# The last 22 expert blocks in another order, transposes of y behind the next first product, and a combine without gates

## The chip, the cores and the metric

The kernel runs on one core of a Trainium2 chip as one launch. The metric is the device time of the launch in microseconds; of the kernel before there are three runs: 2601.29, 2603.02 and 2605.94 us, so the median is 2603.02. A further run was recorded by the hardware profiler and gives all views of the profile below.

## The reference

Four sequences (B = 4) of T = 512 tokens of width C = 512 go through two layers, each with two residual steps:

```python
x = x + mamba2(gate(x))        # layer 0, state space block
x = x + experts(gate(x))       # layer 0, 8 experts, top 2
x = x + attention(gate(x))     # layer 1, 16 heads in 4 groups
x = x + swiglu(gate(x))        # layer 1, 1408 wide, ternary weights
```

`gate` is a bidirectional recurrence over the tokens: two scans forward and two backward (a numerator and a denominator, a*decay + input), whose quotient, scaled, multiplies sigmoid(x). Its inputs besides x are the same for every step, so the quotient (called a gate below) of a layer's step and a batch can be computed before x is there.

The experts: every token gets 8 logits, keeps the two largest, and weights the two experts' outputs by a softmax over the two.

```python
for e in range(E):
    h = x @ w1[e].T + b1[e]
    y = h[:, 0::2] * sigmoid(1.702 * h[:, 0::2]) * (h[:, 1::2] + 1.0)
    out += (y @ w2[e].T + b2[e]) * we[:, None]      # we: 0 where e isn't chosen
```

So a token needs two experts only, and 4 * 512 * 2 = 4096 rows of work are there in all. By these inputs the experts 0 to 7 get 445, 1766, 393, 17, 483, 772, 163 and 57 rows.

## The kernel before

**Blocks.** Rows with one expert are gathered in blocks of 128. There are NBLK = 39 blocks. The first NEARLY = 17 (early blocks) are full blocks of the first three batches to come out of the state space layer, and run beside that layer's last batch. The 22 late blocks hold what is left; FIRST = 15 of them may hold rows of batch 0 and stand ahead of the others, so that batch 0 is complete before the last blocks. `order_blocks` (L604 to L659) makes the lists: from the counts of rows it gives each block in use a rank (the number of used blocks ahead of it, by a product with a triangular matrix), compares that rank with the numbers 0, 1, 2, ... along the free axis (`lane`, L640) and multiplies the one-hot result with token lists and experts. The rank thus is the position in the order of work, and experts stand in the order of their numbers.

**A round.** `Experts.round` (L816 to L839) handles block i: it fetches the rows of block i+3 by an indirect DMA on POOL (`fetch`, L722), asks for weights (`weights`, L745 on, `load_w1` L696 and L701, `load_w2` L707 and L708, all on SP's queue), transposes the rows (`flip`: TensorE `pfl` L734, ACT copies `hT` L736), runs the first product (`pg` L763), the down product of block i−2 (`po` L796, then DVE L801 and a scatter of rows on POOL, L802), transposes the next block's rows, and runs the second product (`pn` L774). Between them ACT and DVE make y (tanh L121, DVE L768, L778, L780, L781). `finish` transposes y (`pyt` L787) and ACT copies it to `yT` (L789), which the down product reads. All products are fp32 with 512 columns; each of four matmuls appears in the trace as two records.

**Weights.** An expert's load is two halves of w1 (1 MB each), b1 (0.5 MB), w2 (1 MB) and b2 (0.25 MB). Early blocks use one buffer set (slot 0). Late blocks alternate two slots by the block's number (`slot`), block 17 on slot 1, block 18 on slot 0. A load is conditional: it moves nothing where the slot holds the expert already.

```python
kw = {"cond": e != self.held[s]} if s in self.held else {}
```

**Gates.** `make_gates` and `gate_pair` (L218 to L364) compute the gates of layer 1 for two halves of the features at a time, a pair, as a generator. `pump` runs one step of it; `more` (L1464) calls it after each round, and attention calls `nudge` in every head. A batch's gate must be whole when `gated` needs it; whatever is missing is made then.

**Order.** The program's text gives most of the order on each engine; a recording layer merges what stands under `after(...)` into the streams named there, where it fits. Behind block 31 `load_group(0)` puts attention's first weights on SP's queue (L1418, L1424). The results of batch 0 are read back by POOL (`rr`, L1435), scaled and added on ACT (L1442) and DVE (L1443), transposed (`pcb`, L1448) and added to x (L1452), one quarter of 128 tokens in each of four of the last five rounds (L1480 to L1488). Batches 1 to 3 are combined the same way in the first heads of attention (L1643 to L1645), where SP issues the reads. Attention starts with keys `pk` (L1530).

Of the kernel before, what the change touches and what calls it, by code (L numbers as in the profile page):

```python
# [10 lines left out]
F32 = mybir.dt.float32  # L11
I32 = mybir.dt.int32
AF = mybir.ActivationFunctionType
ALU = mybir.AluOpType
# [3 lines left out]
P = 128  # L18
B, T, C = 4, 512, 512
NC = C // P  # L20
NT = T // P
# [14 lines left out]
NBLK = (B * T * TOPK + E * (P - 1)) // P  # L36
NROW = B * T * TOPK + 1

NEARLY = -(-((B - 1) * T * TOPK - E * (P - 1)) // P)

FIRST = (T * TOPK + E * (P - 1)) // P
# [39 lines left out]
def block_kernel(ctx: ExitStack, tc: tile.TileContext, a: dict, out: bass.AP):  # L81
    nc = tc.nc

    @contextmanager
    def after(*engines):

        with ExitStack() as es:
            for e in engines:
                last = next(
                    (i for i in reversed(nc.cur_bb.bb.instructions) if i.engine == e.engine), None  # L90
                )
                if last is not None:
                    es.enter_context(tc.issue_after(last))
            yield
# [39 lines left out]
    rt = ctx.enter_context(tc.tile_pool(name="moe_r", bufs=1))  # L134
    tmp = ctx.enter_context(tc.tile_pool(name="tmp", bufs=2))
# [23 lines left out]
    def row(name):  # L159
# [10 lines left out]
                            pattern=[[1, P]], channel_multiplier=-1)  # L170
    tri_gt = const.tile([P, P], F32, name="tri_gt")
    nc.gpsimd.affine_select(out=tri_gt, in_=ones, compare_op=ALU.is_gt, fill=0.0, base=0,
                            pattern=[[-1, P]], channel_multiplier=1)
# [5 lines left out]
    th = const.tile([P, B], F32, name="th")  # L179
# [189 lines left out]
    def pump(n=1, until=None):  # L369
        for _ in range(n):  # L370
            while until not in made and not next(making, True):
                pass
# [18 lines left out]
    def gated(l, b, xb, pool, part=slice(0, T), **kw):  # L391
# [23 lines left out]
                            pattern=[[1, E], [-1, E]], channel_multiplier=0)  # L415
# [3 lines left out]
                            pattern=[[1, P]], channel_multiplier=-1)  # L419
# [3 lines left out]
                            pattern=[[-NQ, E]], channel_multiplier=1)  # L423
    nc.gpsimd.affine_select(out=sel, in_=sel, compare_op=ALU.is_ge, fill=0.0, base=NQ - 1,
                            pattern=[[NQ, E]], channel_multiplier=-1)

    def count(name, pattern, mult=0, base=0):
        n = 1
        for _, k in pattern:
            n *= k  # L430
        ti = tmp.tile([P, n], I32, tag="th", name=f"{name}_i")
        nc.gpsimd.iota(ti, pattern=pattern, base=base, channel_multiplier=mult)
        tf_ = rt.tile([P, n], F32, name=name)
        nc.vector.tensor_copy(tf_, ti)
        return tf_

    lane = count("lane", [[1, P]])

    res_id = [count(f"res{c}", [[TOPK * T, B], [P, NT]], 1, 1 + c * T) for c in range(2)]
    for r in res_id:  # L440
        for b in (0, B - 1):
            rb = r[:, b * NT : (b + 1) * NT]
            nc.vector.tensor_scalar(rb, rb, float(AT[b] - b * TOPK * T), None, ALU.add)
    e_nq = count("e_nq", [[NQ, E]])
    v_id = count("v_id", [[1, 1]], 1)

# [157 lines left out]
    def order_blocks(lo, hi):  # L604

        n = hi - lo
        cv = rt.tile([P, 1], F32, tag="cv", name="cv")
        nc.vector.tensor_tensor(jk, sel, cnt[:, (N2 if lo else N2 - NT), :], ALU.mult)
        nc.vector.tensor_reduce(cv, jk, AX.X, ALU.add)
        use = rt.tile([P, 1], F32, tag="use", name="use")  # L610
        if lo == 0:
            nc.vector.scalar_tensor_tensor(use, v_lo, float(P), cv, ALU.add, ALU.is_le)
        else:
            nc.vector.tensor_tensor(use, v_lo, cv, ALU.is_lt)
            nc.vector.tensor_tensor(use, use, taken, ALU.subtract)
        pi = ps_tp("pidx")
        rank = rt.tile([P, 1], F32, tag="vrank", name="vrank")
        if lo == 0:
            nc.tensor.matmul(pi[:, P : P + 1], lhsT=tri_lt, rhs=use, start=True, stop=True)
            nc.vector.tensor_copy(rank, pi[:, P : P + 1])  # L620
        else:

            two = rt.tile([P, 2], F32, tag="two", name="two")
            nc.vector.tensor_tensor(jk, sel, cnt[:, NT, :], ALU.mult)
            nc.vector.tensor_reduce(rank, jk, AX.X, ALU.add)
            nc.vector.tensor_scalar(two[:, 0:1], v_lo, rank, use, ALU.is_lt, ALU.mult)
            nc.vector.tensor_tensor(two[:, 1:2], use, two[:, 0:1], ALU.subtract)
            nc.tensor.matmul(pi[:, P : P + 2], lhsT=tri_lt, rhs=two, start=True, stop=True)
            nc.tensor.matmul(pi[:, P + 2 : P + 3], lhsT=ones, rhs=two[:, 0:1], start=True, stop=True)

            nc.vector.tensor_scalar(
                rank, pi[:, P + 1 : P + 2], pi[:, P + 2 : P + 3], two[:, 1:2], ALU.add, ALU.mult
            )
            nc.vector.scalar_tensor_tensor(
                rank, pi[:, P : P + 1], two[:, 0:1], rank, ALU.mult, ALU.add
            )
        if lo == 0:
            nc.vector.scalar_tensor_tensor(taken, rank, float(n), use, ALU.is_lt, ALU.mult)
        of = tmp.tile([P, NBLK], F32, tag="th", name="of")
        nc.vector.tensor_scalar(of[:, :n], lane[:, :n], rank, use, ALU.is_equal, ALU.mult)  # L640
        nc.tensor.matmul(pi[:, :n], lhsT=toks, rhs=of[:, :n], start=True, stop=True)
        nc.tensor.matmul(pi[0:1, 2 * P : 2 * P + n], lhsT=v_e, rhs=of[:, :n], start=True, stop=True)

        gf = tmp.tile([P, NBLK], F32, tag="th", name="gf")
        nc.vector.tensor_scalar(gf[:, :n], pi[:, :n], NROW - 2.0, None, ALU.add)
        nc.vector.tensor_copy(idx_h[:, lo:hi], gf[:, :n])
        low = tmp.tile([P, NBLK], I32, tag="th", name="low")
        nc.vector.tensor_scalar(
            low[:, :n], idx_h[:, lo:hi], T - 1, (B - 1) * T, ALU.bitwise_and, ALU.bitwise_xor
        )  # L650
        nc.vector.tensor_scalar(
            idx_h[:, lo:hi], idx_h[:, lo:hi], 1, (B - 1) * T,
            ALU.logical_shift_right, ALU.bitwise_and,
        )
        nc.vector.tensor_tensor(idx_h[:, lo:hi], idx_h[:, lo:hi], low[:, :n], ALU.bitwise_xor)
        ef = tmp.tile([1, NBLK], F32, tag="th", name="ef")
        nc.vector.tensor_scalar(ef[:, :n], pi[0:1, 2 * P : 2 * P + n], E - 1.0, None, ALU.add)
        nc.vector.tensor_copy(eb[:, lo:hi], ef[:, :n])
        nc.vector.tensor_copy(idx_o[:, lo:hi], pi[:, :n])  # L659

    class Experts:
# [154 lines left out]
        def round(self):  # L816
            i = self.i
            self.fetch(i + self.LOOK)
            if i < NBLK:
                self.weights(i)  # L820
                if i >= NEARLY:
                    self.weights(i + 1)
                self.flip(i)
                half = self.first_half(i)
                next(half)
                if i + 1 < NEARLY:
                    self.weights(i + 1, True)
            if i >= 2:
                self.down(i - 2)
            self.second_weights(i - 2)  # L830
            if i < NBLK:
                self.flip(i + 1)
                self.y[i] = next(half)
                if i + 1 < NEARLY:
                    self.more_weights(i + 1)
            if i - 1 in self.y:
                with after(nc.tensor):
                    self.yT[i - 1] = self.finish(self.y.pop(i - 1))
            self.i += 1  # L839

    moe = Experts()
# [617 lines left out]
    with tc.tile_pool(name="moe_w2", bufs=1, reuse_waits="tile") as wm:  # L1459
        moe.add_slot(wm)  # L1460
        for b in range(B):
            nc.sync.dma_start(out=x[b], in_=xs_d[b])

        def more(limit):  # L1464
            while moe.i < min(limit, moe.known):
                moe.round()
                with after(nc.vector):
                    pump()

        more(moe.i + 1)  # L1470
        next(routing)
        more(moe.i + 1)
        next(routing)
        more(moe.i + 1)
        order_blocks(NEARLY, NBLK)
        moe.know(NBLK)
        more(NBLK - 8)
        first_group = load_group(0)

        more(min(NEARLY + FIRST + 2, NBLK - NT - 1))  # L1480
        results = {t: load_results(0, t, nc.gpsimd) for t in range(2)}
        more(moe.i + 1)
        for t in range(NT):
            more(moe.i + 1)
            with after(nc.tensor, nc.vector, nc.scalar):
                add_results(0, t, results.pop(t))
            if t + 2 < NT:
                results[t + 2] = load_results(0, t + 2, nc.gpsimd)  # L1488
        assert moe.i == NBLK
        early_h = gated(2, 0, x[0], wa, tag="wq", name="h2_0")  # L1490
        moe.round()
        moe.round()
# [281 lines left out]
```

## Time and profile before

| | |
|---|---|
| median of three runs | 2603.02 us |
| profiled execution | 2605.88 us, its span 2604.2 us |
| granted TensorE clock, mean | 0.979 |
| TensorE busy | 2450.3 us, 94% |
| VectorE (DVE) / ScalarE (ACT) / GpSimd (POOL) busy | 1412.3 / 1033.2 / 259.9 us |
| moved by DMA | 259.82 MB, 231.51 MB of it on the queue that SP uses |
| first late block, first product | 897.08 us |
| first matmul of attention | 1185.96 us |

The span is the time from the first to the last record; the launch's own time is some 1.7 us more. Views of the trace give lines of start, length, engine, source line, operation, output and inputs, and in brackets the idle time before it with what ended it. A wait belongs to the instruction that waited; instructions of one engine run in order, so what stands behind a waiting instruction waits too.

### The profile page before, as it was taken

How to read it: one execution, taken by the hardware profiler on the slowest of the kernel's cores; microseconds unless marked ns; L12 is line 12 of the kernel's file. 1: busy time of each engine (PE TensorE's matmuls, PEld its weight loads, DVE VectorE, ACT ScalarE, POOL GpSimd, SP SyncE). 2: the span in 40 equal slices, each digit the busy share in tenths (PEclk: the TensorE clock that was granted, in tenths of full speed). 3: DMA queues.
4: the chain of work that ended last, by engine and by line, in shares of the span. 5: the costliest groups of instructions: out<-in, count | busy, mean ns of one | idle time of the engine just before them, and what ended most of it. 6: DMA issues, size and time to landing. Idle time of an engine off the chain costs nothing.

```text
span 2604.2 us, 24554 instructions
## 1 busy us (share of the span) xinstructions
PE 2450.3 (94%) x8204; PEld 1300.7 (50%) x8204; DVE 1412.3 (54%) x2788; ACT 1033.2 (40%) x2126; POOL 259.9 (10%) x299
## 2 busy tenths in 40 slices
PE   3889998999989999989999999999999999999999
PEld 1555555556544444435555555555555554444444
DVE  8798898996345565556666654556553441011010
ACT  4576757666123233224454444345443431000000
POOL 1031223322211121210000000000000000000000
PEclk9989999999899999999999999999999999999999
DMA  6222423324244697876221101111000012000000
GB/s 216 82 93 94 166 74 126 130 69 146 82 177 170 217 371 296 334 242 219 61 65 45 45 29 29 45 41 33 21 25 16 17 53 97 17 0 16 8 8 16
DMA packets 91391, 259.82 MB, mean 100 GB/s; under 512 B 9857, under 2 KB 19457, under 8 KB 80641
## 3 DMA queue, kind: packets, MB, share of 16 engines
q1 hardware_dynamic: 82080, 231.51, 25.5%
q0 software_dynamic: 6880, 22.55, 2.4%
q10 hardware_dynamic: 2304, 4.20, 0.4%
q8 instruction: 65, 1.06, 0.2%
q14 instruction: 62, 0.50, 0.1%
HBM read 284.82 MB, written 47.05 MB: 127 GB/s over the span
## 4 chain that ended last, share of the span: by engine, by line
PE 77%; DVE 14%; ACT 4%; DMA 3%; issue 2%; POOL 0%; SPq 0%; ACTq 0%; DVEq 0%; POOLq 0%
PE pd L1616 8%; PE pq L1552 7%; PE pfu L1683 6%; PE pfo L1693 6%; PE pfg L1678 6%; PE pctx L1601 5%; PE pn L774 5%; PE pg L763 5%; PE po L796 4%; PE pc L995 4%; PE psc L1569 3%; PE po L1223 3%; PE pv L1538 2%; PE ptp L1592 2%; PE pk L1530 2%; PE pz L1066 2%
## 5 line engine op out<-in xcount | busy, mean ns | idle before, releaser
L1552 PE MATMUL pq<-h,wq 128*128 128x512 f32 x512 | 249.4, 603 | 9.5 <-ACT pr L1579 9.4
L1616 PE MATMUL pd<-cx,wd 128*128 128x512 f32 x512 | 222.4, 592 | 0.0
L995 PE MATMUL pc<-h,wxb 128*128 128x512 f32 x320 | 150.0, 624 | 45.8 <-DVE h L1263 38.7
L1687 ACT ACTIVATE hd<-pfg,cols 128x512 f32<-128x512 f32 x44 | 30.3, 688 | 381.0 <-PE pfg L1678 381.0
L1688 DVE SCALAR_TENSOR_TENSOR hd<-pfu,cols,hd 128x512 f32<-128x512 f32 x44 | 33.0, 751 | 269.2 <-PE pfu L1683 269.1
L1572 DVE TENSOR_TENSOR psc<-psc,mask 128x128 f32<-128x128 f32 x256 | 71.7, 287 | 196.1 <-PE psc L1569 196.0
L1579 ACT ACTIVATE pr<-psc,nmax 128x128 f32<-128x128 f32 (+3 forms) x256 | 135.3, 529 | 98.1 <-DVE nmax L1574 97.3
L1601 PE MATMUL pctx<-pT,v 128*128 128x512 f32 (+3 forms) x512 | 155.9, 448 | 7.5 <-ACT pT L1595 4.0
L1683 PE MATMUL pfu<-h,ffu 128*128 128x512 f32 x352 | 158.7, 592 | 0.9 <-DMA ffu<-in_upT 0.9
L1678 PE MATMUL pfg<-h,ffg 128*128 128x512 f32 x352 | 158.6, 592 | 0.0
L796 PE MATMUL po<-w,yT 128*128 128x512 f32 x312 | 145.3, 607 | 12.7 <-ACT yT L789 12.7
L1569 PE MATMUL psc<-kT,qT 128*128 128x128 f32 (+3 forms) x512 | 151.8, 436 | 2.2 <-ACT qT L1560 1.2
L1616 PEld LDWEIGHTS pd<-cx,wd 128*128 128x128 f32 x512 | 96.1, 190 | 114.8 <-issue 110.5
L1693 PE MATMUL pfo<-hd,ffd 128*128 128x512 f32 x352 | 151.7, 592 | 0.0
L763 PE MATMUL pg<-w,hT 128*128 128x512 f32 x312 | 145.1, 605 | 6.7 <-DMA w<-in_w1x 6.7
L1601 PEld LDWEIGHTS pctx<-pT,v 128*128 128x128 f32 x512 | 94.6, 193 | 99.2 <-issue 37.4
L774 PE MATMUL pn<-w,hT 128*128 128x512 f32 x312 | 141.0, 593 | 1.7 <-DMA w<-in_w1x 1.7
L1624 DVE TENSOR_TENSOR xr<-xr,pd 128x512 f32<-128x512 f32 x64 | 44.0, 688 | 175.5 <-PE pd L1616 175.5
L1574 DVE TENSOR_REDUCE nmax<-psc 128x1 f32<-128x128 f32 (+3 forms) x256 | 123.4, 484 | 2.7
L1552 PEld LDWEIGHTS pq<-h,wq 128*128 128x128 f32 x512 | 87.8, 193 | 68.4 <-issue 57.4
L1592 PEld LDWEIGHTS ptp<-ident,pr 128*128 128x128 f32 x640 | 78.3, 143 | 86.9 <-issue 40.4
L995 PEld LDWEIGHTS pc<-h,wxb 128*128 128x128 f32 x320 | 61.8, 199 | 118.2 <-issue 73.0
(305 smaller groups left out, 4217.4 us busy)
## 6 DMA issues: line engine op xcount, KB each, us to landing
w<-in_w1x SPq DMA_DIRECT2D x80, 1024.0 KB
w<-in_w2x SPq DMA_DIRECT2D x40, 1024.0 KB
wb<-in_b1x SPq DMA_DIRECT2D x40, 512.0 KB
lm<-cs SPq DMA_DIRECT2D x32, 512.0 KB
kt<-in_fT SPq DMA_DIRECT2D x62, 256.0 KB
ek<-ek SPq DMA_DIRECT2D x62, 256.0 KB
ekv<-ekv SPq DMA_DIRECT2D x62, 256.0 KB
g<-num SPq DMA_DIRECT2D x30, 512.0 KB
```

Of the source, the lines that this page charges most:

```text
L763: nc.tensor.matmul(pg, lhsT=hT[:, k, :], rhs=self.w1[s][0][:, k, :], start=(k == 0), stop=(k == NC - 1))
L774: nc.tensor.matmul(pn, lhsT=hT[:, k, :], rhs=self.w1[s][1][:, k, :], start=(k == 0), stop=(k == NC - 1))
L796: nc.tensor.matmul(po, lhsT=yT[:, j, :], rhs=self.w2[s][:, j, :], start=(j == 0), stop=(j == NI - 1))
L995: nc.tensor.matmul(pc, lhsT=wxb[:, k, m * P : (m + 1) * P], rhs=h[:, k, :], start=(k == 0), stop=(k == NC - 1),)
L1552: nc.tensor.matmul(pq, lhsT=u.wq[:, k, i * KVC : (i + 1) * KVC], rhs=u.h[:, k, :], start=(k == 0), stop=(k == NC - 1),)
L1569: nc.tensor.matmul(psc[:, :n], lhsT=qT[:, qi * P : n], rhs=u.kT[:, :n], start=True, stop=True)
L1579: nc.scalar.activation(pr, psc[:, :n], AF.Exp, bias=nmax, accum_out=rsum)
L1601: nc.tensor.matmul(pctx[:, kj * P :], lhsT=u.v[:, kj, :], rhs=pT[:, kj, kj * P :], start=(kj == 0), stop=(kj == NT - 1),)
L1616: nc.tensor.matmul(po, lhsT=u.wd[:, i, m * P : (m + 1) * P], rhs=u.ctxT[i], start=(i == 0), stop=(i == HPG - 1),)
L1678: nc.tensor.matmul(pg, lhsT=wg[:, k, cs], rhs=h[:, k, :], start=(k == 0), stop=(k == NC - 1))
L1683: nc.tensor.matmul(pu, lhsT=wu[:, k, cs], rhs=h[:, k, :], start=(k == 0), stop=(k == NC - 1))
L1693: nc.tensor.matmul(po, lhsT=wdn[:, i, m * P : (m + 1) * P], rhs=hd[i], start=(i == 0), stop=(i == NFF - 1),)
```

## The change

1. `places` and `place` are new: a list of 22 numbers that is compared with the ranks of the late blocks instead of 0, 1, 2, ... . Where position p held rank p, now positions 0 to 14 hold the ranks 0,8,1,9,2,10,3,11,4,12,5,13,6,14,7, and positions 15 to 21 the ranks 15,19,16,20,17,21,18. One rank list thus goes to the even, one to the odd positions, and these are the two slots. Two iotas on POOL and one copy on DVE make the list at the start of the kernel.
2. The transposes of y of block i−1 (`finish`) move from the end of the round to just behind the first product of block i, in early and late rounds alike.
3. `more` no longer pumps gates after the last rounds (blocks 34 to 38): five steps fewer there, which is the work of one pair. The pairs are made later instead, by attention's calls.

As the streams stand in the built programs, TensorE's late rounds change from `pyt(i-1), pfl(i+1 or i), po(i-2), pg(i), pn(i)` to `po(i-2), pg(i), pyt(i-1), pfl(i+1), pn(i)`, the early ones from `pfl, pg, po, pn, pyt` to `pg, pyt, po, pfl, pn`; the four `pcb` of batch 0 stand behind two or three of a down product's four matmuls instead of before or within other products; and on DVE and ACT one pair's instructions leave the tail and stand in the stretch of attention's heads 9 to 10.

```diff
--- before.py
+++ after.py
@@ -441,6 +441,16 @@
+    places = tmp.tile([P, NBLK], I32, tag="th", name="places")
+    for lo, hi in ((0, FIRST), (FIRST, NBLK - NEARLY)):
+        half = (hi - lo + 1) // 2
+        nc.gpsimd.iota(places[:, lo : lo + 2 * half], pattern=[[1, half], [half, 2]], base=lo,
+                       channel_multiplier=0)
+    place = rt.tile([P, NBLK - NEARLY], F32, name="place")
+    nc.vector.tensor_copy(place, places[:, : NBLK - NEARLY])
     e_nq = count("e_nq", [[NQ, E]])
     v_id = count("v_id", [[1, 1]], 1)
@@ -637,7 +647,9 @@
         of = tmp.tile([P, NBLK], F32, tag="th", name="of")
-        nc.vector.tensor_scalar(of[:, :n], lane[:, :n], rank, use, ALU.is_equal, ALU.mult)
+        nc.vector.tensor_scalar(
+            of[:, :n], place if lo else lane[:, :n], rank, use, ALU.is_equal, ALU.mult
+        )
@@ -825,6 +837,9 @@
                 if i + 1 < NEARLY:
                     self.weights(i + 1, True)
+            if i - 1 in self.y:
+                with after(nc.tensor):
+                    self.yT[i - 1] = self.finish(self.y.pop(i - 1))
             if i >= 2:
                 self.down(i - 2)
             self.second_weights(i - 2)
@@ -833,9 +848,6 @@
                 if i + 1 < NEARLY:
                     self.more_weights(i + 1)
-            if i - 1 in self.y:
-                with after(nc.tensor):
-                    self.yT[i - 1] = self.finish(self.y.pop(i - 1))
             self.i += 1
@@ -1464,8 +1476,9 @@
             while moe.i < min(limit, moe.known):
                 moe.round()
-                with after(nc.vector):
-                    pump()
+                if moe.i < NBLK - NT:
+                    with after(nc.vector):
+                        pump()
```

## The prediction

> **What bounds the kernel now.** I read the page first, then the windows of the stage that the change touches, then TensorE's waits there, one round, and the chain of work around the two long waits.
>
> ```profile
> PE 2450.3 (94%) x8204; PEld 1300.7 (50%) x8204; DVE 1412.3 (54%) x2788; ACT 1033.2 (40%) x2126; POOL 259.9 (10%) x299
> q1 hardware_dynamic: 82080, 231.51, 25.5%
> PE 77%; DVE 14%; ACT 4%; DMA 3%; issue 2%; POOL 0%; SPq 0%; ACTq 0%; DVEq 0%; POOLq 0%
> ```
>
> TensorE is the bound; only its idle or slowed time can be won. The stage concerned runs from the first product of block 17 (897.08 us) to attention's first `pk` (1185.96): 288.9 us. Its dense content is 22 rounds of first, second and down product (3.43 us each from start to start) and two sets of transposes (0.44 each), about 11.17 us a round as in the early rounds, plus the edge pieces: 254.7 us. So 34.2 us are lost there. In the next view the columns are window, length, then busy us of PE, PEld, DVE, ACT, POOL, the clock, the DMA share and GB/s:
>
> ```profile
> 931.00:1062.00 131.00, 128.00 (x359) 60.52 (x358) 77.58 (x98) 41.26 (x59) 24.64 (x23) 1.00 0.88 342
> 1062.00:1090.00 28.00, 23.35 (x57) 10.45 (x56) 8.49 (x13) 9.48 (x11) 2.98 (x3) 0.88 1.01 382
> 1132.00:1186.00 54.00, 40.27 (x116) 18.63 (x115) 25.96 (x33) 14.64 (x23) 6.45 (x9) 0.94 0.64 222
> ```
>
> TensorE's waits in the stage (total us, times, longest):
>
> ```profile
> PE po L796 <- ACT yT L789: 12.7, 21, 5.4
> PE pcb L1448 <- DVE rr L1443: 5.8, 4, 1.9
> PE pg L763 <- DMA w<-in_w1x: 4.4, 1, 4.4
> ```
>
> One ordinary late round: the transposes of y, those of the next block's rows, and then a down product that needs ACT's copy of the first (columns: start, us, engine, line, operation).
>
> ```profile
> 1000.32 0.60 PE L787 MATMUL pyt<-ident,u 128*128 128x128 f32 x4
> 1000.76 0.60 PE L734 MATMUL pfl<-ident,hb 128*128 128x128 f32 x4
> 1001.61 3.70 PE L796 MATMUL po<-w,yT 128*128 128x512 f32 x8 [0.25 <-ACT yT L789]
> 1005.15 3.60 PE L763 MATMUL pg<-w,hT 128*128 128x512 f32 x8
> ```
>
> From `po` to `po` such rounds take 11.69 us (1001.61 to 1013.30) against 11.17: 0.25 us of wait and 0.27 of restart. There are 16 of them. Then the two long stops, in the chain of work (start, us, what):
>
> ```profile
> 1069.84 9.97 DMA w<-in_w1x
> 1079.81 0.04 issue
> 1079.85 6.45 PE pg L763 x8
> ...
> 1147.04 10.08 DMA rr<-rows_o
> 1157.12 0.02 issue
> 1157.15 0.04 ACTq L1442
> 1157.18 0.05 issue
> 1157.23 0.72 ACT rr L1442
> ```
>
> **What the Trainium skill says.** "TensorE: Matmul & The Clock Gate", section "HAM oscillation — how this bites in real kernels", warns of idle gaps over some 3.4 us, after which matmuls run at half clock. The trace agrees: after 4.40 us idle `pg` took 6.45 us instead of 3.43, after 5.44 us `po` took 5.89; after 0.25 us 3.70. (In attention 2.03 us idle already cost `pq` 5.40, so the threshold isn't sharp.) "DMA: Bandwidth & Descriptors", section "Issuing engines are not separate DMA queues", says that transfers from all issuers interleave on the same 16 engines. It agrees: the results' read `rr` took 10.08 us behind a weights load, its median is 3.7. Its section "Bandwidth" has 1 MB alone at 6.15 us; no load here is alone, and 9.97 us stands for one in a full queue.
>
> **Part 1, fewer loads.** By the routing of these inputs the late blocks' experts in order of rank are 3,5,6,7,0,0,1,1,1,1,2,2,4,4,5 and then 5,5,5,5,6,7,7 (the trace's issue times of the conditional loads agree). Slots alternate by position. Before, 16 of 22 positions find another expert in their slot. Interleaved, the order is 3,1,5,1,6,2,7,2,0,4,0,4,1,5,1 and then 5,6,5,7,5,7,5: 12 loads, at blocks 17,18,19,21,22,23,25,26,29,30,33,35. An expert is 3.93 MB (two w1 halves, w2, two biases), so q1 should fall by 15.7 MB, and nothing loads after block 35.
> - Block 32 (its slot holds expert 5 since block 30) loads nothing: the wait of 4.40 and the slow `pg` (6.45−3.43) go: −7.4 us. The cover for attention's wq and wkv reads, which stood ahead of that load in SP's queue, isn't needed until 1186.
> - Block 18, skipped before, now loads: SP comes to it at 901.31, among w2 of 16 (904.14) and w1 of 19 (906.18). Its `pg` is due at 908.26, `pn` at 912.1, w2 of 16 at about 915. At the 300 GB/s or so of that stretch (280 in the window) w1 lands about 907.4 and 910.8, and w2 of 16 about 916.7: 0 to 5 us lost, I take +2. Behind these three in SP's queue stands only the gate's write at 915.82 and w1 of 19's second half at 916.58, due after 923, so a delay there goes no further.
> - Early waits on w1 (2.3 at 861.96, 1.7 at 870.75) aren't touched by routing; the denser order may fill 0.9 us of the second.
>
> **Part 2, transposes of y behind the next first product.** Late order before: `pyt(i−1), pfl, po(i−2), pg, pn`; after: `po(i−2), pg(i), pyt(i−1), pfl, pn(i)`. Then a copy to yT (0.6 us) has `pfl` and `pn` (3.9 us) before the `po` that may wait for it; `u` has `po` and `pg` (6.9 us) after `pn`, and needs 1.4 on DVE. No instruction more. 16×(0.25+0.27) = −8.2, one longer wait (0.85 at 1125.93) −0.85. In the early rounds (`pfl, pg, po, pn, pyt` to `pg, pyt, po, pfl, pn`), dense before, `u` has 3.4 us of `pg` for 1.4 of DVE; one gate instruction of 1.3 ahead still fits: 0.
>
> **Part 3, no gates in the last five rounds.** Each pump there issues a fifth of one gate pair. Durations by the groups of DVE in the stage: four forward scans at 1.21, four backward at 1.27, six at 0.69, then 1.20, 1.28 and 1.20: 17.7 us of DVE; ACT 10.2 (three of 1.06 to 1.15, two table loads of 1.28, four of 0.72 and two of 0.72); 2 MB over SP. In the tail (1132 to 1186) 13.7 us are idle, 1.81+0.69+1.44+5.44+1.93+0.69+0.59+1.15, and with the slow `po` (+2.3) and restarts 17.3 are lost. The 5.44 came from ACT: its `rr` scaling waited 13.9 us for the read, with yT behind it. After: no weights' load beside that read (3.7 us, not 10), DVE reaches `rr` 2.1 us after `pn` ends, and `pcb` now stands behind three of `po`'s four matmuls (2.6 us). Only the last `pcb` (behind two, 1.7 us) and the end of `h` should wait: 1.8 us left, so −15.5. Bounds: −17.3, and −8 if one read still comes late.
> - The pair isn't gone. By the counts of scheduled gates the pair that ended at block 38 now falls about attention's heads 9 to 9.5, forced by the combine of the last batch. From 1320 to 1350 DVE is busy 23.4 of 30 us and a `pk` of batch 3 already waits 0.72 us there; the softmax (`nmax`, `pr`) shares the engine. What is late next is `h` of batch 3 and so `pk`. The 30 us window has 6.6 us free, 1280 to 1320 has 14 but in pieces; 17.7 minus what fits gives 2 to 9 us of TensorE idle; I take +6.
> - First head of attention: transposes of probabilities interleave otherwise with scores: ±2, taken +0.5.
>
> **Part 4, the start.** Two more iotas on POOL and a copy on DVE stand ahead of `e_nq`; the chain there already runs over POOL (`skip`, 12.5 to 14.7 us) to DVE, and behind the copy on DVE stand the scans of the first gate: +0.5, up to +1.5.
>
> **Sum.** −7.4 −0.9 −8.2 −0.85 −15.5 = −32.9; +0.5 +2 +6 +0.5 = +9: −23.9. The profiled execution took 2605.88 us (span 2604.2), 2.9 above the median of 2603.02; against itself it gives 2582, against the median 2579.
>
> **Rivals.**
> - The pair hides. From 1350 to 1500 attention leaves DVE idle 36 to 49% of the time (25.4, 30.2 and 31.8 us busy of each 50); if the planner's pumps spread it, the +6 becomes 0 and block 18 arrives in time: −32, 2571. Against it: `have` of the last batch's gate forces it before.
> - Waits move. Six of the first seven positions load now (17,18,19,21,22,23), at 0.76 to 0.88 DMA share already; if w1 or w2 comes 3 us late twice with the clock following (3 us each), and one read of results still stalls ACT (7 us), some 13 us go back: about 2592. For it: block 32's stop came from what stood in SP's queue, which remains in order; against it: 6 loads in a row (19 to 24) ran before without a stop.
> - Slower: the pair as one serial burst ahead of batch 3's `h`. If none of it overlaps: DVE 17.7, ACT 10.2, g's write and read back about 8 (two transfers near 4 us): 36, and slow clock after it 3: 39 instead of 6: +6 against before, 2609. It decides from 33−3 = 30 us of exposed burst on. Against it: TensorE has score and projection work of the other heads ready in order, though only up to `pk`.
> - It doesn't do what it says: if loads stay at 16, part 1's 7.4 us and some of part 3's go: 2590. The experts' order above speaks against it.
>
> **How the numbers follow.** As summed 0.50 (2579, own range 2570 to 2588); pair hidden 0.17 (2571); waits move or loads stay 0.21 (2591); little left after several of these costs 0.06 (about 2600); slower 0.06 (2609). A tenth at each end leaves 2565 to 2599. The three runs before span 4.65 us, so 0.2%, 5.2 us, is about what can be told from no change. Faster means under 2597.8: 0.87; same 0.07; slower 0.06.
>
> **What would show it.** Right: q1 near 215.8 MB; no wait `pg` <- w1 near block 32; `po` <- yT near 0 and rounds of 11.17 us; `pk` starts near 1155; the tail without `rr` waits over 2 us. Then attention longer than before by about 6 us, with the wait at batch 3's `pk`. Wrong: a `pg` or `pn` wait on w1 or w2 at blocks 18 to 23 over 5 us, a `pk` wait of batch 3 over 15 us, or early rounds above 11.2 us.

## The result and the profile after

The changed kernel takes 2590.32 us, median of four runs (2589.60 to 2591.44), beside 2604.48 us for the kernel before on the same chip: a ratio of 0.9938, interval 0.9922 to 0.9955, or 11.7 to 20.3 us less. Forecast were 2579 us and 24 us less: the way was right, the time lies in the range, and the gain is some 60 to 67% of the forecast one (14.2 us by the medians, 16.1 by the ratio).

The page of the changed kernel, the lines that answer to those shown of before:

```profile
PE 2446.0 (94%) x8204; PEld 1301.0 (50%) x8204; DVE 1409.8 (54%) x2786; ACT 1032.3 (40%) x2129; POOL 250.4 (10%) x301
q1 hardware_dynamic: 79200, 215.78, 24.3%
PE 75%; DVE 16%; ACT 4%; DMA 3%; issue 1%; POOL 0%; SPq 0%; ACTq 0%; DVEq 0%
```

q1 moved 215.78 MB, 15.7 MB less, four experts: the loads fell from 16 to 12 as worked out. The rest is read by stages. I cut both profiled executions (spans 2604.2 and 2589.7 us) at the same points: the first expert product, the first product of block 17, the first product of block 34, attention's `pk`, and the first matmul of the last step.

| stage, us | before | after | difference |
|---|---|---|---|
| to the first expert product | 671.5 | 678.0 | +6.5 |
| early blocks | 225.6 | 229.6 | +4.0 |
| late blocks 17 to 33 | 212.6 | 199.3 | −13.3 |
| late blocks 34 to 38 and the combine ("tail") | 76.2 | 58.2 | −18.1 |
| attention | 959.1 | 965.7 | +6.6 |
| last step | 459.1 | 458.9 | −0.2 |

(The cut between the two late rows is where DVE takes up the first product of block 34; the late stage in all is 288.9 and 257.5 us.) The late stage gave 31.4 us, and attention took back 6.6, as forecast; the two stages ahead of them lost 10.5, for which the sum had −0.4 (+0.5 and −0.9).

Windows of the late stage after (columns as before: window, length, busy PE, PEld, DVE, ACT, POOL, clock, DMA share, GB/s), then all of TensorE's waits in it, one ordinary round, and the last block's combine:

```profile
931.00:1062.00 131.00, 130.50 (x371) 62.27 (x370) 79.07 (x100) 40.03 (x58) 25.76 (x24) 1.00 0.83 308
1062.00:1090.00 28.00, 28.00 (x85) 13.79 (x84) 13.55 (x19) 12.27 (x17) 5.53 (x6) 1.00 0.82 283
1112.00:1165.00 53.00, 52.45 (x159) 25.54 (x158) 21.74 (x32) 11.24 (x20) 7.94 (x11) 1.00 0.39 139
```

```profile
PE po L808 <- DMA w<-in_w2x: 1.2, 1, 1.2
PE pcb L1460 <- DVE rr L1455: 0.5, 1, 0.5
PE pg L775 <- DMA w<-in_w1x: 0.5, 1, 0.5
```

```profile
1001.94 3.60 PE L775 MATMUL pg<-w,hT 128*128 128x512 f32 x8
1005.37 0.60 PE L799 MATMUL pyt<-ident,u 128*128 128x128 f32 x4
1005.81 0.60 PE L746 MATMUL pfl<-ident,hb 128*128 128x128 f32 x4
1006.25 3.60 PE L786 MATMUL pn<-w,hT 128*128 128x512 f32 x8
1009.68 3.60 PE L808 MATMUL po<-w,yT 128*128 128x512 f32 x8
...
1159.01 0.63 PE L1460 MATMUL pcb<-ident,rr 128*128 128x128 f32 x4 [0.55 <-DVE rr L1455]
```

TensorE idled 22.9 us there before (12.7 + 5.8 + 4.4) and idles 2.2 now; no clock below 1.00 is left in these windows (0.88 and 0.94 before). The round has no wait at all, the tail's one wait is 0.55 us.

In the early blocks 3.0 of the 4.0 us lost lie between the first products of blocks 13 and 17 (48.7 us before, 51.7 after; 0.4 of it is one set of transposes that falls on the other side of the cut), and there at one place, block 14. Its two products of before, and then the chain of work after (start, us, what):

```profile
861.96 3.70 PE L763 MATMUL pg<-w,hT 128*128 128x512 f32 x8 [2.26 <-DMA w<-in_w1x]
870.75 3.70 PE L774 MATMUL pn<-w,hT 128*128 128x512 f32 x8 [1.66 <-DMA w<-in_w1x]
```

```profile
862.20 1.24 DVE num L328
863.44 0.02 issue
863.46 0.34 SPq L330
...
864.53 6.36 DMA w<-in_w1x
870.89 0.14 issue
871.02 6.64 PE pg L775 x8
```

Block 14's expert goes into the single slot. The slot's first half is free since block 13's first product ended at 859.4, but SP issues the load at 864.53, because the write of a gate (L330) stands ahead in its queue and waits for DVE's last step of that gate. The product waits 3.75 us and then runs at half clock, 6.64 us. Before, the same write held the same load to 856.10 (the slot's half was free at 851.8). So the block waited as long before, 2.26 and 1.66 us, 3.92 in two pieces; what is new is that the wait now stands in one piece and the product behind it is slow.

In attention the work of the pair stands where it was expected, but what it makes late is not `pk` of batch 3: it is above all the results (`rr`) that the combine ahead of it adds.

```profile
1311.27 3.70 PE L1629 MATMUL pd<-cx,wd 128*128 128x512 f32 x8 [0.92 <-DVE xr L1637]
1322.20 3.70 PE L1565 MATMUL pq<-h,wq 128*128 128x512 f32 x8 [1.41 <-ACT pr L1592]
1329.29 0.63 PE L1460 MATMUL pcb<-ident,rr 128*128 128x128 f32 x4 [3.39 <-DVE rr L1455]
```

### The profile page after: what moved, and what is told of

The parts are those of the page before. It is cut to its first block, busy times and chain, and to the rows that moved or that the text cites. A ratio compares the mean times of both kernels' runs of the same rounds, so it can differ in the third digit from the quotient of the medians.

```text
span 2589.7 us, 24584 instructions
## 1 busy us (share of the span) xinstructions
PE 2446.0 (94%) x8204; PEld 1301.0 (50%) x8204; DVE 1409.8 (54%) x2786; ACT 1032.3 (40%) x2129; POOL 250.4 (10%) x301
## 3 DMA queue, kind: packets, MB, share of 16 engines
q1 hardware_dynamic: 79200, 215.78, 24.3%
## 4 chain that ended last, share of the span: by engine, by line
PE 75%; DVE 16%; ACT 4%; DMA 3%; issue 1%; POOL 0%; SPq 0%; ACTq 0%; DVEq 0%
PE pd L1629 8%; PE pq L1565 7%; PE pfu L1696 6%; PE pfo L1706 6%; PE pfg L1691 6%; PE pctx L1614 5%; PE po L808 5%; PE pg L775 5%; PE pn L786 5%; PE psc L1582 3%; PE pc L1007 2%; PE po L1235 2%; PE pv L1551 2%; PE ptp L1605 2%; PE pz L1078 2%; PE pk L1543 2%
```

## The experiments

All times below are ratios to the kernel before on the same chip, with 95% intervals; us of difference are the ratio's share of 2605. The stages come from one profiled execution each, and identical code differs between profiles: by up to 9 us ahead of the first expert product and by up to 4 in the early stage (below). First each part alone.

**The order of blocks alone** (the diff's first two hunks).

```diff
+    place = rt.tile([P, NBLK - NEARLY], F32, name="place")
+    nc.vector.tensor_copy(place, places[:, : NBLK - NEARLY])
...
+            of[:, :n], place if lo else lane[:, :n], rank, use, ALU.is_equal, ALU.mult
```

> The kernel before with the interleaved list of late blocks alone; transposes of y and gates stay. Theory A (the three parts add up as in the sum): q1 falls to 215.8 MB, the stop of block 32 (7.4 us) goes, the late read of results shrinks from 10 to about 4 us (5 to 7 us), block 18 costs up to 2: the late stage from the first product of block 17 to attention's first product takes 276 to 280 us instead of 288.9, attention stays at 959 us. Theory B (the waits on weights move elsewhere): the late stage stays over 284 us, with new waits on w1 or w2 at blocks 18 to 23. Theory S (the two iotas and the copy at the start shift the state space stage): the first expert product starts near 678 us instead of 671.5. Theory N (that shift is chance): near 671 or scattered.

Measured: 0.9950 (0.9934 to 0.9966), −13.0 us. Late stage 276.3 us, as theory A had it: 5.9 us of the 12.6 gained lie in the tail, whose late read of results now has no load of an expert beside it (it lands in 4.1 us). Attention 958.8. First expert product at 673.6, so neither 671 nor 678.

**The transposes of y alone.**

```diff
+            if i - 1 in self.y:
+                with after(nc.tensor):
+                    self.yT[i - 1] = self.finish(self.y.pop(i - 1))
             if i >= 2:
                 self.down(i - 2)
...
-            if i - 1 in self.y:
-                with after(nc.tensor):
-                    self.yT[i - 1] = self.finish(self.y.pop(i - 1))
```

> The kernel before with the transposes of y behind the next first product alone. Theory A: the 16 rounds fall from 11.69 to 11.17 us, and in the tail the transposes leave ACT's reach of the late read, so the late stage takes 277 to 281 us instead of 288.9 (8.2 of rounds, up to 4 of the 5.4 us stop); block 32's stop of 4.4 us stays or grows, since the round ahead of it is shorter. Rival B: the shorter rounds ask for weights earlier and the queue can't follow, so half of the 8 us comes back as waits on w1 and the late stage takes 284 us or more. Early expert stage: 225.6 us as before (A) or 2 to 4 us more (the move costs in the early rounds, as the whole change showed 229.6). The first expert product is at 671.5 by theory S, since the start isn't touched, or scattered by theory N.

Measured: 1.0028 (1.0016 to 1.0039), 7.3 us slower. The late stage takes 290.8 us: rival B. The 16 small waits are gone, but blocks 17 to 33 keep only 2.8 us of that, and the tail loses 4.7. The time stands elsewhere, in TensorE's waits of this run's late stage:

```profile
PE pcb L1448 <- DVE rr L1443: 8.4, 4, 3.4
PE pg L763 <- DMA w<-in_w1x: 8.3, 4, 6.2
PE po L796 <- ACT yT L789: 6.7, 2, 6.0
```

```profile
1082.26 6.23 PE L763 MATMUL pg<-w,hT 128*128 128x512 f32 x8 [6.25 <-DMA w<-in_w1x]
```

With 16 loads still to come, block 32 waits 6.25 us for its weights where it waited 4.40. The early blocks take 227.8 us. (The profiled execution was the fastest of ten, 2607.4 us; the median is 2612.8, so the stages show less than the whole loss.)

**No gates in the tail alone.**

```diff
-                with after(nc.vector):
-                    pump()
+                if moe.i < NBLK - NT:
+                    with after(nc.vector):
+                        pump()
```

> The kernel before without gates after the last five rounds alone. Theory A: the tail loses the waits for DVE (pcb 5.8 us in four) but not the 5.4 us behind the late read of results nor the 1.15 and 0.69 at yT: the late stage takes 282 to 285 us instead of 288.9; attention takes 965 to 967 us instead of 959.1 because the pair is made there; together the time is within 3 us of before. Rival P (the gates in the tail were hidden): late stage 287 to 289 and the whole 6 us slower. First expert product at 671.5 (S) or scattered (N).

Measured: 0.9975 (0.9964 to 0.9986), −6.5 us. The late stage takes 273.9 us, 8 less than expected: the 5.4 us stop is gone too, with all 16 loads still there.

```profile
PE po L796 <- ACT yT L789: 7.7, 21, 0.7
PE pg L763 <- DMA w<-in_w1x: 4.1, 1, 4.1
```

No `pcb` waits, no wait for yT is over 0.75 us, and the last read of results is issued at 1140.1 instead of 1147.0. Attention takes 967.6 us, 8.5 more.

**The start alone**: the list counts 0, 1, 2, ... so that the order stays.

```diff
-        nc.gpsimd.iota(places[:, lo : lo + 2 * half], pattern=[[1, half], [half, 2]], base=lo,
+        nc.gpsimd.iota(places[:, lo : lo + 2 * half], pattern=[[2, half], [1, 2]], base=lo,
```

> The kernel before with the two iotas and the copy at the start and the list used in the comparison, but counting 0, 1, 2, ..., so that the order of blocks stays as before. Theory S (the work at the start shifts the state space stage against TensorE's clock): first expert product near 678 us instead of 671.5 and the whole 6 to 8 us slower than before. Theory N (chance): the first expert product stays at 669 to 674 us and the time within 3 us of before.

Measured: 1.0002 (0.9994 to 1.0010), 22 runs: theory N by the time. The first expert product of the profiled execution is at 677.1, where theory S had it, and yet the median is that of before. Over all 14 profiles it is at 668.9 to 678.0; the mean is 673.3 us in the ten with the edit at the start and 672.9 in the four without.

Then the whole change less one part.

**The changed kernel with the transposes back at the round's end.**

```diff
-            if i - 1 in self.y:
-                with after(nc.tensor):
-                    self.yT[i - 1] = self.finish(self.y.pop(i - 1))
             if i >= 2:
                 self.down(i - 2)
...
+            if i - 1 in self.y:
+                with after(nc.tensor):
+                    self.yT[i - 1] = self.finish(self.y.pop(i - 1))
```

> The changed kernel with the transposes of y put back at the end of the round (interleaved list and no gates in the tail stay). Theory A (the move is worth the 0.25 + 0.27 us of 16 rounds once loads and gates are out of its way): the late stage takes 266 to 268 us instead of 257.4, and the early expert stage 224 us instead of 229.6, so the whole is 2 to 5 us slower than the changed kernel, at 2593 to 2596. Rival B (the move alone gave nothing, so it gives nothing here): the late stage stays within 2 us of 257.4 and the whole is 3 to 5 us faster than the changed kernel, since the early rounds gain.

Measured: 0.9953 (0.9936 to 0.9970), −12.2 us. Late stage 268.0, early stage 225.0: theory A. So the move is worth 10.6 us in the late stage here and minus 4.6 in the early one, where alone it was worth nothing.

**The transposes moved in late rounds only.**

```diff
-            if i - 1 in self.y:
+            if i >= NEARLY and i - 1 in self.y:
                 with after(nc.tensor):
                     self.yT[i - 1] = self.finish(self.y.pop(i - 1))
...
+            if i - 1 in self.y:
+                with after(nc.tensor):
+                    self.yT[i - 1] = self.finish(self.y.pop(i - 1))
```

> The changed kernel with the transposes of y moved in late rounds only; early rounds keep the order of before. Theory E (the move costs in the early expert stage, where the load of the single slot's first half follows the first product and now has less work between): early stage 223 to 226 us instead of 229.6, the whole 3 to 5 us faster than the changed kernel, 2585 to 2588. Theory N (the 229.6 is chance of the clock and of SP's waits): 228 to 231 and no difference.

Measured: 0.9908 (0.9890 to 0.9927), −24.0 us, 2581.89 us. Early stage 223.5 us, late stage 257.4, as in the changed kernel: theory E by the stages. The runs gain 8 us on the changed kernel by the ratios, more than the 3 to 5 expected and than the 6 of the early stage. (This profiled execution was the fastest of six, 2574.3 us, with the first expert product at 668.9, the earliest of all; stages ahead of the early one are not compared.)

**The changed kernel with five more steps of gates ahead of the tail.**

```diff
-                        pump()
+                        pump(2 if moe.i in (21, 25, 28, 29, 32) else 1)
```

> The changed kernel with five more steps of gates in late rounds ahead of the tail (after blocks 20, 24, 27, 28 and 31, where no expert is loaded), so that the pair that fell about head 9 of attention is whole at block 33. Theory A: attention takes 958 to 960 us instead of 965.7, the late stage 257 to 259; the whole is 5 to 7 us faster than the changed kernel, 2583 to 2586. Rival D (DVE can't hide ten steps in these rounds): the late stage grows by 4 us or more, by waits for yT and u in the five rounds, and the gain is gone. Rival F (attention's 6.6 us aren't from the pair): attention stays at 964 to 967.

Measured: 0.9960 (0.9945 to 0.9974), −10.4 us, 6 us behind the changed kernel. Attention takes 959.8 us, so its 6.6 are the pair (against rival F); the tail stays at 58.2. But blocks 17 to 33 grow by 21.8 us. Rival D has the size and not the mechanism: TensorE waits for w1 more than for yT (first view), and SP waits long before a gate's reads of keys (L237 and L246) and its writes (L330) (second view, what SP waits for in this stage). The second view alone proves nothing: such waits are 81.0 us here, but 68.7 in the changed kernel, whose late stage loses only 0.5 us to w1. The run below with all of these transfers on POOL's queue tests it.

```profile
PE pn L786 <- DMA w<-in_w1x: 8.1, 3, 3.6
PE po L808 <- ACT yT L801: 4.2, 1, 4.2
PE pg L775 <- DMA w<-in_w1x: 2.1, 2, 1.8
```

```profile
SPq L719 <- PE po L808: 42.0, 11, 10.4
SPq L246 <- DVE num L256: 36.7, 5, 9.6
SPq L237 <- DVE eu L275: 31.6, 4, 12.0
...
SPq L330 <- DVE num L328: 12.7, 3, 9.0
```

**The changed kernel with the writes of layer 1's gates on POOL's queue.**

```diff
-            nc.sync.dma_start(out=gts[l][b][:, c0 : c0 + 2, :], in_=g)
+            queue = nc.gpsimd if l >= 2 else nc.sync
+            queue.dma_start(out=gts[l][b][:, c0 : c0 + 2, :], in_=g)
```

> The changed kernel with the writes of layer 1's gates on POOL's queue instead of SP's, where a write waits for DVE's last step of a gate (L328 before) ahead of the loads of w1. Theory Q (that wait holds up the load of block 14's or 15's w1 in the single slot: 3.75 us idle at 871 and a first product at half clock after it): the wait goes, the early stage takes 222 to 225 us instead of 229.6, the whole is 4 to 7 us faster than the changed kernel. Rival R (the load itself is late, its slot being free only after the first product): the wait stays over 2 us and the early stage over 227.

Measured: 0.9898 (0.9878 to 0.9917), −26.6 us, 2581.00 us; by the ratios 10 us ahead of the changed kernel, more than the 4 to 7 expected. Early stage 223.7: theory Q. SP now issues block 14's load at 852.82, as soon as block 13's first product has left the slot, with w2 and the second half in turn, and the product (860.37) starts without a wait; 1.49 us remain at the second one.

```profile
860.37 3.60 PE L776 MATMUL pg<-w,hT 128*128 128x512 f32 x8
863.80 0.60 PE L800 MATMUL pyt<-ident,u 128*128 128x128 f32 x4
864.24 3.60 PE L809 MATMUL po<-w,yT 128*128 128x512 f32 x8
867.68 0.60 PE L747 MATMUL pfl<-ident,hb 128*128 128x128 f32 x4
869.77 3.70 PE L787 MATMUL pn<-w,hT 128*128 128x512 f32 x8 [1.49 <-DMA w<-in_w1x]
```

**Both of these edits.** The changed kernel with the writes on POOL's queue and with the transposes moved in late rounds only.

> The changed kernel with both single edits that gained: transposes of y moved in late rounds only, and writes of layer 1's gates on POOL's queue. Theory A (the two act on different losses of the early stage, the rounds and the wait for w1): early stage 220 to 222 us, late 256 to 257, attention 964 to 968; about 2577 to 2580. Rival (both remove the same wait): early 223 to 224 as each alone, 2580 to 2582.

Measured: 0.9899 (0.9884 to 0.9914), 2577.50 us. Early stage 220.7, late 256.3, attention 964.3, as theory A has it. The early stage is a weak witness: the last experiment has the same early code and takes 224.4, all of the difference ahead of block 13. From there to block 17 the two agree, 44.7 and 44.8 us, with no wait on w1 left, beside 47.9 with the order put back alone and 46.5 with the write moved alone: that is theory A. By the ratio it can't be told from either edit alone, −26.3 us (22.4 to 30.2) against −24.0 and −26.6. It is faster than the kernel before by 27.8 us of medians; its interval ends below where that of the changed kernel begins.

**The kernel with both edits, and all of layer 1's gate transfers on POOL's queue, and the five steps spread.**

```diff
+        queue = nc.gpsimd if l >= 2 else nc.sync
...
-            nc.sync.dma_start(out=kt[i], in_=a["fT"][cc * P : (cc + 1) * P, b, :])
+            queue.dma_start(out=kt[i], in_=a["fT"][cc * P : (cc + 1) * P, b, :])
...
-                nc.sync.dma_start(out=ek[i], in_=eks[b][:, cc, :])
+                queue.dma_start(out=ek[i], in_=eks[b][:, cc, :])
...
-                nc.sync.dma_start(out=ekv[i], in_=ekvs[b][:, cc, :])
+                queue.dma_start(out=ekv[i], in_=ekvs[b][:, cc, :])
...
+                        pump(2 if moe.i in (21, 25, 28, 29, 32) else 1)
```

> The same with all of layer 1's gate transfers (reads of keys and writes of gates) on POOL's queue and the five further steps of gates in late rounds as in the run that spread them. Theory Q (spreading failed because the gates' reads and writes wait in SP's queue ahead of the loads of w1): the late stage returns from 279 to 257 to 263 us and attention keeps 959 us, about 2572 to 2578. Rival V (DVE is full in those rounds and delays y): the late stage stays over 268 us, with waits for yT instead of w1. Rival W (POOL's own queue blocks, row fetches and scatters stand behind the gates' waits): waits for the rows of a block (pfl) or late results.

Measured: 0.9896 (0.9879 to 0.9912), 2577.42 us. The late stage returns from 279.3 to 264.3, attention keeps 960.9: mostly theory Q, with 1.3 us more than its range and some of V, since what is left are waits of that kind (TensorE, late stage):

```profile
PE po L809 <- ACT yT L802: 3.7, 3, 3.0
PE pg L776 <- ACT hT L749: 2.3, 2, 1.3
```

Against the kernel with both edits it takes 3.4 us from attention and puts 8.0 on the late rounds; the median is the same, so nothing is won.

**The kernel before with four pairs of buffers for the results of batch 0.**

```diff
-            r = cb.tile([P, C], F32, tag=f"rr{c}", name=f"rr{c}", bufs=2)
+            r = (pool or cb).tile([P, C], F32, tag=f"rr{c}", name=f"rr{c}", bufs=2)
...
-        results = {t: load_results(0, t, nc.gpsimd) for t in range(2)}
+        results = {t: load_results(0, t, nc.gpsimd, wm if t >= 2 else None) for t in range(NT)}
...
-            if t + 2 < NT:
-                results[t + 2] = load_results(0, t + 2, nc.gpsimd)
```

> The kernel before with four pairs of buffers for the results of batch 0 instead of two, so that all eight reads are issued together and none waits until DVE has added the one before. Gates stay in the tail. Theory B (the 5.4 us stop and the slow product after it came from the late release of the buffer, which the gates on DVE delay): the stop goes and the late stage takes 279 to 282 us instead of 288.9, attention stays at 959; the whole 7 to 9 us faster. Rival C (DVE's own delay of rr and y, not the read, makes most of the tail's 17 us): 285 to 289, the whole at most 4 us faster.

Measured: 0.9979 (0.9969 to 0.9989), −5.5 us; late stage 283.0, 5.8 less, between the two ranges. The stop itself went as theory B says; first the down product of before, then the same one here and what follows:

```profile
1159.49 5.89 PE L796 MATMUL po<-w,yT 128*128 128x512 f32 x8 [5.44 <-ACT yT L789]
```

```profile
1156.33 3.70 PE L796 MATMUL po<-w,yT 128*128 128x512 f32 x8 [0.69 <-ACT yT L789]
1159.87 1.02 PE L763 MATMUL pg<-w,hT 128*128 128x512 f32 x2
1163.82 0.63 PE L1448 MATMUL pcb<-ident,rr 128*128 128x128 f32 x4 [2.93 <-DVE rr L1443]
```

But the next `pcb` waits 2.93 us for DVE where it had waited 1.93.

**Both edits, with gates in the tail again and the four pairs of buffers.**

```diff
-                if moe.i < NBLK - NT:
-                    with after(nc.vector):
-                        pump()
+                with after(nc.vector):
+                    pump()
```

> The kernel with both gaining edits, with the gates pumped in the tail again as before and four pairs of buffers for the results. Theory B: without the late read gates in the tail cost 3 to 6 us there (waits for DVE's rr), attention falls from 966 to 959, so it ends 2 to 5 us ahead of the kernel with both edits. Rival C: the tail costs 8 us or more, and nothing is gained.

Measured: 0.9915 (0.9901 to 0.9928), 2581.76 us, some 4 us behind both edits alone: rival C. The tail takes 70.2 us instead of 58.2, 9.3 of it in waits of `pcb` for DVE's `rr`; attention gains 8.5 (955.8). So by these two profiles the gates cost 3.5 us more in the tail than in attention; the runs agree (2577.50 and 2581.76), though the intervals of the two ratios overlap.

## Why the prediction was right, and where it was not

Of the two profiles' difference of 14.5 us, 9.4 are missing from the forecast 23.9: the early blocks cost 4.9 more than forecast and the stretch ahead of them 6.0, while the late stage gave 1.5 more, and attention came out as forecast.

**Fewer loads (−7.4, block 18 +2): right.** 12 loads, 215.78 MB. The stop of block 32 is gone in every run with the new order and stays in every one without it. In place of block 18's 2 us there are 1.2 us on w2 at 927.05, in the round of block 19.

**Transposes of y in late rounds (−9.05): right in size, wrong as a thing of its own.** In the full change it is worth 10.6 us (268.0 against 257.5). Alone it gave nothing: the prediction added it to the sum as if it needed no cover, but the time saved was lost again to waits for weights and in the tail. Which of the other two parts it needs, the fewer loads, the quiet tail or both, was not tested apart. The three parts alone are worth 12.6, −2.0 and 15.0 us of the late stage, 25.6 in sum; done together they are worth 31.4.

**No gates in the tail (−15.5): right in size, its reason half right.** I put the 5.4 us stop down to the weights' load beside the read of results. With the gates away and all loads kept it is gone; with the loads away and gates kept the last read lands in 4.1 us and no wait for yT is over 1.15; with more buffers and neither edit it is gone. So the stop took both: POOL issued the read late while the gates on DVE delayed the work ahead of it, and the read then met the load. Either edit was enough to end it, so the two parts can't be given shares of it.

**The pair in attention (+6, and +0.5 for the first head): right in size, wrong in place.** +6.6 in the two profiles. Over the runs, attention takes 963.7 to 968.0 us in the six with the pair there and 954.8 to 961.8 in the eight without. What is late is the combine's `rr`, not `pk` of batch 3 (a wait of 3.39 us, with 0.92, 1.41 and others around it).

**Early rounds (0) and early waits (−0.9): the step that failed.** This term was +4. What I did reckon with held: `u` has time enough, and the dense early rounds stay at 11.18 us. I left out what the order does to the wait for block 14's weights. In the kernels where SP writes the gates, the three with the new early order take 227.8, 227.8 and 229.6 us and the seven with the old one 223.3 to 225.7. In the three, block 14's first product waits 3.24 to 3.75 us in one piece and then takes 5.2 to 6.6 us; in the seven it waits 2.1 to 2.3 us, and is slowed in one of them only.

The gate's write in SP's queue holds that load in either order, so it is not by itself what the new order cost. From the first product of block 13 to that of block 17 (us; the new order's figures hold 0.4 of the cut):

| | SP writes the gates | POOL writes them |
|---|---|---|
| old early order | 47.4 to 48.7 (seven, mean 48.1) | 44.7, 44.8; 46.4 with the reads there too |
| new early order | 49.7, 49.8, 51.7 | 46.5 |

In this stretch the write costs 3 to 5 us in either order; the new order, less the 0.4, costs 1.3 where POOL writes and 1.2 to 3.1 where SP does, most where the product behind the wait is slowest. Putting the order back or moving the write gained 6 us each in the early stage and 8 to 10 by the ratios; the rest may be the stretch ahead of the experts, the next term. Some 1 us of the +4.0 lies ahead of block 13, within the spread of the same code (176.0 and 179.6 in two profiles), and its cause stays open. That the first `pk` stood at 1165 and not near 1155 is this term and the next one.

**The start (+0.5): not to be told from nothing.** −1.6 to +2.6 us. The 6.5 us that the profile shows ahead of the experts are not the edit, as far as is known: with the same edit alone the ratio is 1.0002. They are differences of the granted clock, whose mean up to the first expert product is 0.950 before and 0.940 after; length times what is missing to 1 is 33.7 and 40.5 us, 6.8 apart. One place makes 2.5 us, the same `pc` in the timelines, first before, then after:

```profile
172.90 2.82 PE L995 MATMUL pc<-h,wxb 128*128 128x512 f32 x6
```

```profile
175.61 5.33 PE L1007 MATMUL pc<-h,wxb 128*128 128x512 f32 x6
```

Whether the changed kernel falls on the late side of this spread more often than the others stays open; it had four runs. By stages without it the gain would be 21 us, just beyond the far end of the measured interval.

The rivals: waits did not move in the full change's late stage, but did in the part alone, by the mechanism given. The serial burst didn't come: 6.6 us, far from 30. Two sums of the rivals were off: the burst of 39 us would have cost +9 against before, 2612 us, not +6 (the +2 and the two +0.5 were left out), and the waits that move, as described, add up to 19 us, not 13.

## What to carry to other kernels

The time of a small wait that is removed is kept only if what feeds the next step is early enough already; so test such an edit beside the one that makes its feed early, not only alone. Follow the queue that issues transfers: a write that waits for its producer holds every load behind it, though the write itself takes 0.34 us. When an instruction moves, ask also whether two short waits become one long one: here 3.9 us in two pieces left the clock alone, and 3.75 in one piece did not. Work taken out of a busy stretch has to be paid where it goes, so price both places: one gate pair cost 12.0 us in the tail, in the two profiles that differ by it, and 7 in attention, between the means of the profiles with and without it.

## What was not expected of the hardware

- The time up to the first expert product varies from 668.9 to 678.0 us between profiled executions whose products there are the same, by stretches of products at half clock (`pc` 5.33 us instead of 2.82; the mean clock of that stretch is 0.954 in the earliest profile and 0.940 in the latest). Two profiles can thus differ by 9 us for no reason of the code. Stages cut behind that point differ less, but the early stage still by 3.7 us with the same code (220.7 and 224.4).
- The Trainium skill's "DMA: Bandwidth & Descriptors", section "Issuing engines are not separate DMA queues", has it that issuing from several engines saves only the sequencer's issue time. Here the move of one write (0.34 us to issue) from SP to POOL let SP issue block 14's load at 852.82, when its slot came free, instead of 5 us after that, and took the early stage from 229.6 to 223.7 us: the write's wait for DVE no longer held SP's loads. The measurement decides.
- Idle time of one length did not always slow the clock. In all fourteen profiles a `pq` in attention's first head comes after 2.03 us of idle time; in eight its sixth record then starts 3.6 to 3.95 us after its first, in six 2.25 us after it. In the expert blocks all fifteen waits of 2.96 to 6.25 us ahead of six or more unbroken records of a product were followed by slow ones; of the seven of 2.07 to 2.34 us one was (2.34, then 5.40 us instead of 3.70).
